# Three PSUM tiles in place of one: weighted values, second layer's narrow half and projection, with the pairs of banks in another order

## Chip, cores and metric

One Trainium2 chip (trn2), one core. The metric is the device time of one execution in microseconds, median of several executions.

In the profile PE is TensorE, which does the matmuls; DVE is VectorE, ACT ScalarE and POOL GpSimd. PEld stands for PE's weight loads. The matmuls write into PSUM, which is handled in banks. The granted clock is the share of TensorE's full clock that the trace shows as granted. A line such as `PE s L92 <- ACT o L536: 88.6, 62, 1.5` says that PE, about to write tile s at line 92 of the kernel, waited for ACT's operation on o at line 536: 88.6 us in total, 62 times, 1.5 us at most.

## What is computed

The reference works on x of shape 16 x 192 x 56 x 56 (float32). Cut to what matters here:

```python
# layer 0: shifted-window attention (7x7 windows, 6 heads of 32) and a two-layer perceptron
h   = roll(ln(x^T), (-3, -3));  win = windows(h)                   # 49 tokens each
q, k, v = split(win @ qkv_w + qkv_b)
out = softmax(q k^T * scale + bias + mask) v @ proj_w + proj_b
x1  = x + roll(unwindow(out), (3, 3))^T
x2  = x1 + (gelu(ln(x1^T) @ fc1_w + fc1_b) @ fc2_w + fc2_b)^T
# layer 1: depthwise 3x3 convolution, of which 4 taps are not masked; the taps depend on the image
t   = relu(bn(mean(x2, (2, 3)) @ w1.T));  wt = t @ w2.T + b2
out = depthwise_conv(x2, wt * MASK) + bias
```

The 192 channels are handled as 128 + 64. The "wide half" of a result is that of the 128 channels, the "narrow half" that of the 64. Each of the 64 steps handles one band of windows in two halves of the image, and four steps make an image.

## The kernel before

The kernel uses eight banks of PSUM as four pairs, each a tile of two banks, and the loop passes the pairs round under the names A, B_, C and D. All operations are issued in the order of the program. `mm` is the helper at line 92, so nearly all matmuls carry that line; tell them apart by their tiles (ph: first layer, pf: second layer, po: weighted values, pp: projection, pv: values of the next step, s: the shared tile).

```python
def banks(name, k):                       # one tile = one pair of banks
    return psum.tile([128, 2, 512], F32, tag=f"pair{k}", name=name)

def bank(k):
    return singles[0][:, k]
...
def attention_values(i, prts, k):
    po = banks(f"po_{i}", k)
    for wp in range(4):
        attention_weigh(po, bank(1), wp, prts[wp])      # a third of it into bank(1)
    return po[:, 0], po[:, 1], bank(1)

def project(i, o, k):
    pp = banks(f"pp_{i}", k)
    pp1 = bank(1)                                       # narrow half
    ...
def mlp_narrow(hid, pf1):  ...                          # second layer, narrow half
def taps(b, pooled):
    pt = bank(0)  ...                                   # taps of the convolution
```

The part of a step that the change touches (`mlp_out` is DVE's sum into x at L631, `conv_rest` the convolution's operations on DVE, `attention_rows` ACT's copies of the weighted values at L536):

```python
    pf = mlp_wide(i - 2, hid, B_, turn)
    mlp_out(i - 2, 0, pf[:, :, :T])
    ...
    singles[0] = banks(f"s_{i}", C)                     # the shared tile
    if has(i):
        o = attention_rows(i, attention_values(i, prts, D))
    mlp_narrow(hid, bank(0))
    for c in ys:
        conv_rest(*c)
    mlp_out(i - 2, 1, bank(0)[:, :T])
    if has(i):
        pp, pp1, p_narrow, p_rest, p_whole = project(i, o, A)
        p_narrow()
        p_rest()
    if has(i + 1):
        pvs, v_rest, v_whole = attention_v(i + 1, (B_, D))
        v_rest()
    if (i - 2) % STEPS == STEPS - 1:
        ...  taps(b, taps_pool(b))
    if has(i):
        p_whole()
        residual(i, pp, pp1)
    if has(i + 1):
        v_whole()
        attention_v_out(pvs)                            # copies that free the values' banks
    ...
    pairs = [C, A, B_, D]
```

## Time and profile before

| | before |
|---|---|
| median time | 3428.45 us (4 runs) |
| PE busy in the profiled run | 3183.9 us of 3430.2, 93% |
| PE idle | 246.3 us |
| of it: waits on the shared tile in the loop | 145.3 us |

The last row is the sum of 88.6 (on ACT o), 52.2 (on DVE's L631) and 4.5 us (on the taps' tt). PE busy and PE idle together are the span. The windows of two successive steps, from one narrow projection to the next (length, then busy time of PE, of its weight loads, of DVE, ACT and POOL, each with its number of instructions, then the granted clock, the share of DMA and its GB/s):

```profile
1705.35:1756.44 51.09, 48.76 (x415) 29.95 (x415) 34.30 (x60) 29.20 (x47) 11.46 (x10) 1.00 0.12 33
1756.44:1807.34 50.90, 48.76 (x414) 29.94 (x414) 25.85 (x54) 27.50 (x45) 11.70 (x11) 1.00 0.25 71
```

PE does the same 48.76 us of work in each step and idles for the rest.

### The profile page before, as it was taken

The page shows a single profiled execution, that of the slowest core. Times are in us where ns is not written, and L with a number is a line of the kernel's source. Part 1 is how long each engine was busy: PE and PEld are TensorE (multiplying, and loading weights), DVE is VectorE, ACT ScalarE, POOL GpSimd, SP SyncE. Part 2 cuts the span into 40 slices and gives each one's busy share as a digit, 9 for nine tenths or more (in the row PEclk, how much of TensorE's full clock was granted, in tenths as well). Part 3 has the DMA queues.
Part 4 walks back from the last instruction along what each step waited for, and adds up shares of the span by engine and source line. Part 5 has one row for each costly group of instructions (what it writes and reads, how often), then busy time and mean ns, then how long its engine had stood idle before and what let it go on. Part 6 is the DMA issues. An engine that isn't in the chain of part 4 may idle for free.

```text
span 3430.2 us, 64894 instructions
## 1 busy us (share of the span) xinstructions
PE 3183.9 (93%) x26642; PEld 1955.5 (57%) x26642; DVE 2078.5 (61%) x3893; ACT 1854.5 (54%) x2988; POOL 759.8 (22%) x656
## 2 busy tenths in 40 slices
PE   5799999999999999999999999999999999999996
PEld 3455555555555555555555555555555555555553
DVE  4354675665665665665665666665665656666564
ACT  3354564565565565565565565565565565555552
POOL 4211212212212212212212212212212222222220
PEclk7799999999999999999999999999999999999998
DMA  3101102111111102101111201102111110201001
GB/s 94 19 10 48 29 25 57 34 48 34 51 27 38 53 26 61 29 27 55 34 51 31 59 23 35 53 29 58 29 30 52 34 54 28 62 22 32 25 29 43
DMA packets 79124, 135.39 MB, mean 39 GB/s; under 512 B 21766, under 2 KB 61692, under 8 KB 76908
## 3 DMA queue, kind: packets, MB, share of 16 engines
q1 hardware_dynamic: 77266, 128.54, 13.3%
q8 instruction: 210, 3.44, 0.4%
q0 software_dynamic: 1056, 1.92, 0.3%
q10 hardware_dynamic: 506, 0.79, 0.1%
q14 instruction: 86, 0.70, 0.1%
HBM read 41.25 MB, written 38.54 MB: 23 GB/s over the span
## 4 chain that ended last, share of the span: by engine, by line
PE 84%; ACT 7%; DVE 4%; issue 1%; POOL 0%; DMA 0%; SPq 0%; DVEq 0%; POOLq 0%; ACTq 0%
PE ph L92 23%; PE pf L92 15%; PE s L92 10%; PE pv L92 7%; PE st L92 5%; PE pq L92 4%; PE pp L92 4%; PE sc L92 4%; PE pe L92 4%; PE pk L92 4%; PE pt L500 3%; ACT o L536 2%; ACT prt L506 2%; ACT L235 2%; DVE y L688 2%
## 5 line engine op out<-in xcount | busy, mean ns | idle before, releaser
L92 PE MATMUL ph<-yn,wf 128*128 128x392 f32 (+1 forms) x3072 | 802.3, 498 | 6.1 <-ACT vbd L443 3.3
L487 POOL TENSOR_TENSOR prob<-e,tot 113x588 f32<-113x588 f32 x256 | 297.8, 1174 | 1966.6 <-DVE tot L486 1966.6
L92 PEld LDWEIGHTS ph<-yn,wf 128*128 128x128 f32 (+1 forms) x3072 | 429.4, 189 | 350.6 <-issue 87.2
L443 ACT COPY vbd<-pv 49x192 f32<-49x192 f32 x512 | 135.4, 312 | 888.7 <-DVE vbd L441 888.5
L92 PE MATMUL pf<-hid,wf 128*128 128x392 f32 x1536 | 538.3, 494 | 3.5 <-ACT hid L588 2.0
L688 DVE SCALAR_TENSOR_TENSOR y<-x,wt,y 128x770 f32<-128x770 f32 x288 | 328.1, 1141 | 288.1 <-ACT y L673 281.4
L588 ACT ACTIVATE hid<-ph,f1b 128x784 f32<-128x784 f32 x384 | 336.8, 912 | 137.7 <-PE ph L92 137.7
L92 PEld LDWEIGHTS pf<-hid,wf 128*128 128x128 f32 x1536 | 281.5, 190 | 183.7 <-ACT hid L588 3.3
L92 PE MATMUL s<-hid,wf 128*64 128x392 f32 x1536 | 266.9, 496 | 88.6 <-ACT o L536 88.6
L92 PEld LDWEIGHTS pv<-wqkv,win 64*128 64x128 f32 (+1 forms) x2048 | 259.7, 190 | 39.6 <-ACT kbd L393 2.8
L471 DVE TENSOR_TENSOR e<-sc,bias_t 113x588 f32<-113x588 f32 x256 | 179.5, 761 | 168.0 <-PE sc L92 167.8
L92 PE MATMUL pv<-wqkv,win 64*128 64x192 f32 (+1 forms) x2048 | 274.0, 327 | 3.3 <-ACT kbd L393 2.5
L478 DVE TENSOR_TENSOR e<-e,top 113x588 f32<-113x588 f32 x256 | 266.5, 1041 | 8.9
L338 POOL TENSOR_TENSOR yn<-x,dv 128x784 f32<-128x784 f32 x64 | 132.0, 2063 | 565.4 <-DMA dv<-dev 537.8
L235 ACT ACT_TABLE_LOAD x192 | 246.3, 1283 | 3.4
L506 ACT COPY prt<-pt 128x678 f32<-128x678 f32 x256 | 179.1, 726 | 117.5 <-PE pt L500 116.0
L481 ACT ACTIVATE e<-e 113x588 f32<-113x588 f32 x256 | 176.8, 691 | 108.7 <-DVE e L478 108.7
L92 PEld LDWEIGHTS s<-hid,wf 128*64 128x64 f32 x1536 | 104.5, 137 | 216.2 <-issue 119.9
L441 DVE COPY vbd<-pv 49x192 f32<-49x192 f32 x512 | 159.1, 349 | 97.0 <-ACT vbd L443 83.0
L500 PEld LDWEIGHTS pt<-ident,prob 113*128 113x128 f32 x1536 | 167.3, 142 | 74.4 <-issue 45.3
L500 PE MATMUL pt<-ident,prob 113*128 113x113 f32 x1536 | 182.7, 262 | 10.3 <-ACT prt L506 8.5
L92 PE MATMUL po<-prt,vbd 128*64 128x49 f32 x4096 | 191.5, 225 | 0.2 <-ACT prt L506 0.2
(157 smaller groups left out, 4688.9 us busy)
## 6 DMA issues: line engine op xcount, KB each, us to landing
dv<-dev SPq DMA_DIRECT2D x1020, 49.0 KB
x<-in_x_dram SPq DMA_DIRECT2D x15, 1484.0 KB
out_dram<-y SPq DMA_DIRECT2D x48, 392.0 KB
out_dram<-y SPq DMA_DIRECT2D x48, 196.0 KB
x<-in_x_dram SPq DMA_DIRECT2D x16, 392.0 KB
x<-in_x_dram SPq DMA_DIRECT2D x15, 350.0 KB
out_dram<-y SPq DMA_DIRECT2D x16, 308.0 KB
out_dram<-y SPq DMA_DIRECT2D x16, 154.0 KB
```

The lines of the kernel that those rows point to most:

```text
L92: nc.tensor.matmul(dst, lhs, rhs, start=start, stop=stop, skip_group_check=True)
L235: nc.scalar.activation(junk, eps_t[0:1], func)
L441: nc.vector.tensor_copy(dst, f)
L443: nc.scalar.copy(dst, f)
L471: nc.vector.tensor_tensor(e, sc[:PW, :, : HEADS * N], rel, ALU.add)
L478: nc.vector.tensor_tensor(ehs[wp], ehs[wp], t.broadcast_to([PW, 2 * HEADS, N]), ALU.subtract)
L481: nc.scalar.activation(es[wp], es[wp], AF.Exp)
L487: nc.gpsimd.tensor_tensor(prob[wp][:PW, :, 0:N], ehs[wp], t.broadcast_to([PW, 2 * HEADS, N]), ALU.mult)
L500: nc.tensor.transpose(pt[:, a, g * PW : (g + 1) * PW], prob[wp][:PW, h : h + 2, :].rearrange("p h k -> p (h k)"), ident[:PW, :PW],)
L506: nc.scalar.copy(prt, pt[:, :, : 3 * PW])
L588: nc.scalar.activation(hid[:, f], phs[f][:, :, :T], AF.Gelu, bias=f1b[:, f : f + 1])
L688: nc.vector.scalar_tensor_tensor(dst, src, wt[:, kc, t : t + 1], dst, ALU.mult, ALU.add)
```

## The change

The intent is to take away the two waits of PE per step that come from one tile serving three purposes. The weighted values' third part (po1), the second layer's narrow half (pf1) and the narrow projection (pp1) each get a tile. So that there are pairs for them, the wide projection moves from A to B_, the next step's values from (B_, D) to (D, A), the taps behind the values, and the pairs go round in another order. The core of the diff:

```diff
-    def attention_values(i, prts, k):
-        po = banks(f"po_{i}", k)
+    def attention_values(i, prts, k, k1):
+        po, po1 = banks(f"po_{i}", k), banks(f"po1_{i}", k1)[:, 0]
...
-    def project(i, o, k):
-        pp = banks(f"pp_{i}", k)
-        pp1 = bank(1)
+    def project(i, o, k, k1):
+        pp, pp1 = banks(f"pp_{i}", k), banks(f"pp1_{i}", k1)[:, 0]
...
-    def mlp_narrow(hid, pf1):
+    def mlp_narrow(i, hid, k):
+        pf1 = banks(f"pf1_{i}", k)[:, 0]
...
-    def taps(b, pooled):
-        pt = bank(0)
+    def taps(b, pooled, k):
+        pt = banks(f"t_{b}", k)[:, 0]
...
-        singles[0] = banks(f"s_{i}", C)
         if has(i):
-            o = attention_rows(i, attention_values(i, prts, D))
-        mlp_narrow(hid, bank(0))
+            o = attention_rows(i, attention_values(i, prts, D, C))
+        pf1 = mlp_narrow(i - 2, hid, A)
...
-            pp, pp1, p_narrow, p_rest, p_whole = project(i, o, A)
+            pp, pp1, p_narrow, p_rest, p_whole = project(i, o, B_, C)
...
-            pvs, v_rest, v_whole = attention_v(i + 1, (B_, D))
+            pvs, v_rest, v_whole = attention_v(i + 1, (D, A))
             v_rest()
-        if (i - 2) % STEPS == STEPS - 1:
-            convs.append({"b": b, "n": 0, "wt": taps(b, taps_pool(b))})
         if has(i):
             p_whole()
             residual(i, pp, pp1)
         if has(i + 1):
             v_whole()
+        if (i - 2) % STEPS == STEPS - 1:
+            convs.append({"b": b, "n": 0, "wt": taps(b, taps_pool(b), C)})
+        if has(i + 1):
             attention_v_out(pvs)
...
-        pairs = [C, A, B_, D]
+        pairs = [C, B_, D, A]
```

(Cut: the two steps of the prologue, where the same tiles are separated in pair 3, and lines that only pass the new names on.)

More of the change, by code (lines that the diff above doesn't have):

```diff
@@ L523, in attention_weigh @@
                 )
-    def attention_values(i, prts, k):
-        po = banks(f"po_{i}", k)
+    def attention_values(i, prts, k, k1):
+        po, po1 = banks(f"po_{i}", k), banks(f"po1_{i}", k1)[:, 0]
         for wp in range(4):
-            attention_weigh(po, bank(1), wp, prts[wp])
-        return po[:, 0], po[:, 1], bank(1)
+            attention_weigh(po, po1, wp, prts[wp])
+        return po[:, 0], po[:, 1], po1
     def attention_rows(i, pos):
@@ L613, in mlp_narrow @@
                 )
+        return pf1
     def mlp_wide(i, hid, k, turn):
@@ L747, in tail_of @@
         if o is not None:
-            pp, pp1, narrow, rest, whole = project(i, o, kp)
+            pp, pp1, narrow, rest, whole = project(i, o, kp, 3)
             narrow()
@@ L949, in tile_swin_then_dynamic_conv @@
             f()
+        if i:
+            singles[0] = banks("singles", 3)
         for e in extra:
@@ L958, in tile_swin_then_dynamic_conv @@
         norm_squares(f"1_{i + 3}", i + 3, 0, nc.gpsimd)
-        o = attention_rows(i, attention_values(i, prts, 0))
+        o = attention_rows(i, attention_values(i, prts, 0, 3))
+        singles[0] = None
         tail_of(i, o, 1, (2, 0))
@@ L1036, in tile_swin_then_dynamic_conv @@
             norm_squares(f"1_{i + 3}", i + 3, 0, nc.gpsimd)
-        singles[0] = banks(f"s_{i}", C)
         if has(i):
-            o = attention_rows(i, attention_values(i, prts, D))
-        mlp_narrow(hid, bank(0))
+            o = attention_rows(i, attention_values(i, prts, D, C))
+        pf1 = mlp_narrow(i - 2, hid, A)
         for c in ys:
             conv_rest(*c)
-        mlp_out(i - 2, 1, bank(0)[:, :T])
+        mlp_out(i - 2, 1, pf1[:, :T])
         if has(i):
-            pp, pp1, p_narrow, p_rest, p_whole = project(i, o, A)
+            pp, pp1, p_narrow, p_rest, p_whole = project(i, o, B_, C)
             p_narrow()
@@ L1048, in tile_swin_then_dynamic_conv @@
         if has(i + 1):
-            pvs, v_rest, v_whole = attention_v(i + 1, (B_, D))
+            pvs, v_rest, v_whole = attention_v(i + 1, (D, A))
             v_rest()
-        if (i - 2) % STEPS == STEPS - 1:
-            b = (i - 2) // STEPS
-            convs.append({"b": b, "n": 0, "wt": taps(b, taps_pool(b))})
         if has(i):
@@ L1058, in tile_swin_then_dynamic_conv @@
             v_whole()
+        if (i - 2) % STEPS == STEPS - 1:
+            b = (i - 2) // STEPS
+            convs.append({"b": b, "n": 0, "wt": taps(b, taps_pool(b), C)})
+        if has(i + 1):
             attention_v_out(pvs)
```

## The prediction

> **What bounds the kernel now.** I read the page first, then the list of waits of TensorE, then PE's timeline in a few steps of the loop, then DVE's beside it. The page:
>
> ```profile
> span 3430.2 us, 64894 instructions
> PE 3183.9 (93%) x26642; PEld 1955.5 (57%) x26642; DVE 2078.5 (61%) x3893; ACT 1854.5 (54%) x2988; POOL 759.8 (22%) x656
> ...
> PE   5799999999999999999999999999999999999996
> ```
>
> PE is busy for 93% of the span, the next engine for 61%, and PE's row is at 9 in nearly all slices. So PE bounds, and only the 3430.2 - 3183.9 = 246.3 us in which it stands idle can be won: the change takes away no matmul and adds none. Who makes PE wait is in the waits of PE:
>
> ```profile
> PE s L92 <- ACT o L536: 88.6, 62, 1.5
> PE s L92 <- DVE x L631: 52.2, 62, 1.2
> PE singles L143 <- DMA cols_rows<-in_L_conv_qkv_b_dram: 10.0, 1, 10.0
> ...
> PE s L92 <- DVE tt L651: 4.5, 15, 0.3
> ```
>
> (columns: total us, times, longest). Two waits come once in each of the 62 loop steps that have an attention, 1.43 us and 0.84 us on average: 140.8 us of the 246. The rest of the list is single waits of the prologue and the end. Both waits are on the tile s: one PSUM tile of two banks that holds the last third of the weighted values (bank 1), the narrow half of the second layer (bank 0) and the narrow half of the projection (bank 1 again). PE's timeline of one step (start us, duration us, group, idle before and releaser):
>
> ```profile
> 1749.66 0.29 PE L92 MATMUL s<-prt,vbd 128*64 128x49 f32 x4
> 1751.43 4.17 PE L92 MATMUL s<-hid,wf 128*64 128x392 f32 x24 [1.48 <-ACT o L536]
> 1756.44 0.88 PE L92 MATMUL s<-o,wp 128*64 128x392 f32 x4 [0.84 <-DVE x L631]
> 1757.25 0.93 PE L92 MATMUL pp<-o,wp 64*128 64x392 f32 x4
> 1758.01 1.47 PE L92 MATMUL pv<-wqkv,win 64*128 64x192 f32 x16
> 1759.41 0.93 PE L92 MATMUL s<-o,wp 128*128 128x392 f32 x2
> 1760.17 1.48 PE L92 MATMUL pp<-o,wp 128*128 128x392 f32 x4
> 1761.48 2.76 PE L92 MATMUL pv<-wqkv,win 128*128 128x192 f32 x16
> ```
>
> The 24 matmuls of the second layer read only hid, ready long ago, and write bank 0. They wait until ACT has copied the weighted values out of bank 1. Then the projection, which needs only o (ACT was done with it 4 us earlier), waits until DVE has read bank 0. Neither wait is of data: both come from the tile being one. A step is about 51 us, and the windows of four successive steps show PE idle for 2.1 to 2.6 us in each, so there is nearly nothing else to win in the loop. The granted clock there is 1.00.
>
> **What the Trainium skill says.** "Perfetto Trace Analysis", section Optimization Strategy, says that a gap which repeats on the engine that should be saturated can mean too few buffers for the next tile; the trace agrees, 62 times each. The same page, section Matmuls, says that independent groups of matmuls should go round different PSUM banks, so that the evacuation of one overlaps the next: here the banks differ, and yet the trace shows the wait, so what counts is the tile that the program tracks. "PSUM — Partial Sum Buffer", section PSUM bank collisions raise a hardware error, asks for order by bank and quadrant, not for order between two banks; so the separated tiles need no wait in its place. "SBUF — State Buffer", section Who interferes with whom, says that a VectorE copy in a two-port mode and a GpSimd operation block each other wholly. The trace agrees: the row copy of the convolution, L697, takes 0.19 us, but 1.72 to 1.84 us when it meets POOL's yn.
>
> **The change, part by part.**
>
> (1) *The second layer's narrow half goes into the step's pair A*, last read by ACT's copy prt of the fourth window pair, which the weighted values need anyway. The wait on ACT o vanishes: 62 x 1.43 = 88.6 us. ACT's copies (1.2 us) then lie beside these 24 matmuls (4.17 us) and are done before the projection.
>
> (2) *The projection goes into B and C.* B was last read by DVE at L631 for the wide half (from 1745.88, 1.03 us: long past), C by ACT o. The wait on DVE vanishes: 62 x 0.84 = 52.2 us. Where groups follow without a wait, the next starts 0.07 to 0.17 us before the end of the one before (pp at 1757.25, s ended at 1757.32). Two such overlaps per step are won back: about 0.2 us x 62 = 12 us. That makes 153 us in all.
>
> (3) *The values of the next step go into D and A.* Their second half is the first thing that must now wait for DVE's L631 on A. PE reaches it the length of the projection's first parts and of half the values later: 0.81 + 0.76 + 0.70 = 2.3 us after the end of the second layer's half. In a step whose convolution has no row copy, DVE is free by then, and L631 takes 0.62 us: no wait. In the steps with a row copy that meets POOL, DVE is late:
>
> ```profile
> 1752.34 1.74 DVE L697 COPY y<-cols 64x56 f32<-64x56 f32 x1
> 1754.12 1.72 DVE L688 SCALAR_TENSOR_TENSOR y<-x,wt,y 128x770 f32<-128x770 f32 x1
> 1755.76 0.61 DVE L631 SCALAR_TENSOR_TENSOR x<-s,cols,x 128x392 f32<-128x392 f32 x1
> ```
>
> L631 ends at 1756.4. PE would be there at 1749.8 (weighted values out) + 4.0 + 2.3 = 1756.1, so it waits some 0.35 us. I counted 11 slow L697 in the loop: 4 us given back.
>
> (4) *The taps of the convolution move behind the values.* This comes in every fourth step, 15 times in the loop (the 16th is in the end). The matmuls themselves are as many. Before, they held the projection up by 0.94 us (1810.31 to 1811.25 in such a step), now they hold up the next step's first ph, which takes the same pair C: much the same. But in DVE's order they now stand before the copies that free the values' banks:
>
> ```profile
> 1810.99 0.21 DVE L651 TENSOR_TENSOR tt<-s,bn 128x48 f32<-128x48 f32 x1 [1.95 <-PE s L92]
> ...
> 1812.74 0.74 DVE L570 SCALAR_TENSOR_TENSOR x<-s,cols,x 128x371 f32<-128x371 f32 x2
> 1813.54 1.41 DVE L574 SCALAR_TENSOR_TENSOR x<-pp,cols,x 128x371 f32<-128x371 f32 x4
> 1814.86 0.60 DVE L441 COPY vbd<-pv 49x192 f32<-49x192 f32 x2
> ```
>
> From tt to the end of the taps is 1.75 us (1810.99 to 1812.74). The copies of the first half then take 2.45 us until ACT's part is done (1814.86 to 1817.31). Set the start of the taps' tt to 0: the pair D is free at 1.75 + 2.45 = 4.2. The first ph starts at about 0.25, and the third, which takes D, 2.64 later (8 matmuls of 0.33), at 2.9. PE waits 1.3 us. The late copies also push ACT's squares and first gelus back, for which the fifth and sixth ph wait a little, 0.3 us. 15 x 1.6 = 24 us given back.
>
> (5) *The new order of the pairs* keeps the roles of the next step: first the pair that the projection's narrow part leaves, then its wide part's, then the values'. The first is free after two DVE operations of 0.75 us in sum, while PE still has 1.3 + 2.6 us of other work. In a usual step the third ph finds its pair free 1.2 us early, before as after. Nothing is won or lost. The two prologue steps separate two tiles in the same pair; nothing.
>
> Sum: 153 - 24 - 4 = 125 us. 3428.9 - 125 = **3303 us**, 3.7% faster (a ratio of 1.038).
>
> **The rivals.** *DVE takes over*: every wait on L631 is only moved from the projection to the second half of the values, and the gain is part (1) and little of (2). For it: in the chain of waits some steps already run over ACT y, DVE y and L631, not over the second layer. Against it: DVE is 61% busy, L631 came at once after the matmuls in 51 of 64 cases (DVE waits 191.9 us there for PE), and PE has 2.3 us of other work first. If it held in the steps with a row copy, 29 x 1 us more would be lost: about 3330 us. *The taps cost nothing or much more*: if the copies keep up, 24 us less is lost and the time is 3280; if the delay runs on through the gelus and the next softmax, 3 us per such step or more, 3325. *Another wait takes the place of the ones removed*, since a step is 2.5 us shorter for all: the DMA of dv to POOL's yn and the next ph is the longest line beside PE. In the trace yn ends at 1860.1 and ph wants it at 1867, so 7 us of room shrinks to 4.5. Were all of the gain eaten, we would be at 3429; I see no sign of it. *The clock is throttled* by a PE that never stops: it is granted 1.00 at 95% already, so I don't expect it.
>
> **Range and chances.** If only the idle of the list is won and not the overlaps, 3316; with no loss at the taps, 3280; with DVE late in the steps with row copies, 3330. So 3280 to 3330 holds it 8 times in 10. Over 2% faster needs 67 us, half of the sum, and part (1) alone has 89: 0.96. Within 2%: 0.035. Slower needs a chain through a new buffer that I don't see: 0.005.
>
> **What would show each step right or wrong.** Right: PE's waits have no line for ACT o and none for L631 before the projection; the second layer's 24 matmuls start as the weighted values end; PE's busy time stays near 3184 and its idle falls to about 120; usual steps take about 48.6 us. Step (3): 11 or so waits of the values on L631, 0.3 us each. Step (4): some 15 waits of ph on ACT or DVE vbd, 1.3 us each, and taps steps 1.6 us longer than the matmuls added. Wrong: waits on L631 before the values in most steps; ph waiting for vbd, yn or the residual in every step; a clock under 1.00 in the loop.

## The result and the profile after

The changed kernel took 3291.36 us (median of 4 runs, 3289.66 to 3292.23), against 3428.45 us before. All outputs are right. Ratios here are the mean time of one kernel's runs over that of the other's runs of the same rounds, so they are not quite the ratio of the medians. This one is 0.9597, with a 95% interval of 0.958 to 0.9614.

The page of the changed kernel:

```profile
span 3290.4 us, 64877 instructions
PE 3164.4 (96%) x26642; PEld 1950.0 (59%) x26642; DVE 2053.2 (62%) x3893; ACT 1856.1 (56%) x2988; POOL 751.3 (23%) x656
```

The matmuls are as many as before (26642). The span fell by 139.8 us. PE's idle fell from 246.3 to 126.0 us, which is 120.3 of it. The other 19.5 us are of PE's busy time, without one matmul less: groups that follow without a wait overlap at their ends (by 0.17 us at each of the two places in the timeline below), and the groups behind a wait had taken 0.04 to 0.05 us longer.

The waits of PE in the changed kernel (total us, times, longest; lines have moved by one, so L632 is the L631 of before):

```profile
PE ph L92 <- ACT vbd L443: 18.8, 16, 3.3
...
PE ph L92 <- DVE tt L652: 5.9, 15, 0.4
PE pv L92 <- DVE x L632: 4.7, 12, 0.5
```

The waits on ACT o and on L631 before the projection are gone from the loop. Three small ones are new in the loop: ph for the copies of the values (one of the 16, 3.3 us long, is in the prologue and was there before), ph for the taps, and the values for L632. The prediction names all three, the second only as "much the same" as the hold-up that it replaces. PE's timeline of a usual step answers to the one that the prediction shows of before:

```profile
1677.45 3.08 PE L92 MATMUL po<-prt,vbd 128*64 128x49 f32 x96
1680.36 4.13 PE L92 MATMUL pf<-hid,wf 128*64 128x392 f32 x24
1684.32 1.69 PE L92 MATMUL pp<-o,wp 128*64 128x392 f32 x8
1685.85 1.47 PE L92 MATMUL pv<-wqkv,win 64*128 64x192 f32 x16
1687.24 2.24 PE L92 MATMUL pp<-o,wp 128*128 128x392 f32 x6
1689.32 2.76 PE L92 MATMUL pv<-wqkv,win 128*128 128x192 f32 x16
```

No line carries an idle in brackets, and each group starts a little before the end of the one above it. The windows of two steps and of a whole image of four steps:

```profile
1544.00:1740.42 196.42, 194.66 (x1664) 120.08 (x1662) 126.39 (x240) 115.21 (x186) 45.47 (x37) 1.00 0.15 42
1594.81:1643.75 48.94, 48.60 (x415) 29.93 (x415) 34.30 (x60) 29.23 (x47) 11.67 (x9) 1.00 0.11 34
1643.75:1692.09 48.34, 48.34 (x415) 29.97 (x415) 32.15 (x60) 29.25 (x47) 11.61 (x9) 1.00 0.18 44
```

A usual step takes 48.34 us, all of it busy, where it took 51.09. In the step of 48.94 us the values waited for L632. Four steps took 205.05 us before (the four pieces of the windows, 51.99 + 51.07 + 51.09 + 50.90) and take 196.42 us now.

What holds PE up in the step with taps shows in DVE's timeline and then in PE's:

```profile
1544.41 0.21 DVE L652 TENSOR_TENSOR tt<-t,bn 128x48 f32<-128x48 f32 x1 [1.09 <-PE t L92]
...
1546.08 0.17 DVE L667 TENSOR_TENSOR wt<-wt,b2t 128x8 f32<-128x8 f32 x1
1546.17 0.61 DVE L441 COPY vbd<-pv 49x192 f32<-49x192 f32 x2
```

```profile
1543.84 0.54 PE L92 MATMUL t<-w1t,pooled 128*128 128x48 f32 x4
1544.77 2.87 PE L92 MATMUL ph<-yn,wf 128*128 128x392 f32 x8 [0.39 <-DVE tt L652]
1548.67 5.90 PE L92 MATMUL ph<-yn,wf 128*128 128x392 f32 x28 [1.03 <-ACT vbd L443]
```

The copies start only at 1546.17, behind the taps' five operations, and the third ph (the ninth matmul) waits 1.03 us for them.

### The profile page after: what moved, and what is told of

It is laid out like the page before. It is cut to its first block, busy times and chain, and to the rows that moved or that the text cites. A ratio compares the mean times of both kernels' runs of the same rounds, so it can differ in the third digit from the quotient of the medians.

```text
span 3290.4 us, 64877 instructions
## 1 busy us (share of the span) xinstructions
PE 3164.4 (96%) x26642; PEld 1950.0 (59%) x26642; DVE 2053.2 (62%) x3893; ACT 1856.1 (56%) x2988; POOL 751.3 (23%) x656
## 4 chain that ended last, share of the span: by engine, by line
PE 88%; DVE 4%; ACT 2%; issue 2%; POOL 0%; DMA 0%; SPq 0%; POOLq 0%; ACTq 0%; DVEq 0%
PE ph L92 23%; PE pf L92 21%; PE pv L92 7%; PE pp L92 7%; PE st L92 5%; PE po L92 5%; PE pq L92 4%; PE pt L500 4%; PE sc L92 4%; PE pe L92 4%; PE pk L92 4%; DVE y L689 1%; DVE y L698 1%; DVE vbd L441 1%; ACT L235 1%
## 5 line engine op out<-in xcount | busy, mean ns | idle before, releaser
L92 PE MATMUL pf<-hid,wf 128*128 128x392 f32 (+1 forms) x3072 | 802.9, 494 | 3.5 <-ACT hid L587 2.0
L92 PEld LDWEIGHTS pf<-hid,wf 128*128 128x128 f32 (+1 forms) x3072 | 386.4, 164 | 303.6 <-issue 119.9
L689 DVE SCALAR_TENSOR_TENSOR y<-x,wt,y 128x770 f32<-128x770 f32 x288 | 320.3, 1114 | 282.1 <-ACT y L674 275.3
L92 PE MATMUL pp<-o,wp 128*128 128x392 f32 (+2 forms) x896 | 251.5, 514 | 2.7 <-ACT o L536 2.7
L632 DVE SCALAR_TENSOR_TENSOR x<-pf,cols,x 128x784 f32<-128x784 f32 (+1 forms) x128 | 105.8, 827 | 233.1 <-PE pf L92 218.9
L235 ACT ACT_TABLE_LOAD x192 | 246.3, 1283 | 3.4
L92 PE MATMUL po<-prt,vbd 128*64 128x49 f32 x6144 | 198.2, 224 | 0.0
L92 PEld LDWEIGHTS po<-prt,vbd 128*64 128x64 f32 x6144 | 190.2, 139 | 9.4 <-ACT prt L506 0.6
```

Source lines behind the costliest of these rows:

```text
L92: nc.tensor.matmul(dst, lhs, rhs, start=start, stop=stop, skip_group_check=True)
L235: nc.scalar.activation(junk, eps_t[0:1], func)
L689: nc.vector.scalar_tensor_tensor(dst, src, wt[:, kc, t : t + 1], dst, ALU.mult, ALU.add)
```

## The experiments

They ran in three sessions, on one chip each, and in each the kernel before ran beside them; its medians there were 3429.5 to 3430.1 us. The change itself had run beside a kernel before of 3428.45 us, so 1 to 2 us between it and another row say nothing. The theory is the prediction's: PE bounds, both waits come from the shared tile and not from data, and small losses are given back. The rivals are that DVE's chain takes over, that the losses have other causes, and that the order of the pairs is free.

| run | median us | ratio to before (95% interval) |
|---|---|---|
| the change | 3291.36 | 0.9597 (0.958 to 0.9614) |
| part (1) alone | 3366.08 | 0.9819 (0.98 to 0.9839) |
| part (1) alone, convolution behind L631 | 3343.45 | 0.9751 (0.9735 to 0.9767) |
| part (2) alone | 3362.4 | 0.9802 (0.9785 to 0.9818) |
| change, taps at their old place | 3269.67 | 0.9533 (0.9518 to 0.9547) |
| change, taps' DVE work split | 3268.54 | 0.9527 (0.9513 to 0.9541) |
| change, taps beside the projection | 3259.4 | 0.9502 (0.9488 to 0.9516) |
| change, row copy on ACT | 3285.61 | 0.9581 (0.9567 to 0.9595) |
| change, taps beside, row copy on ACT | 3252.96 | 0.9485 (0.9471 to 0.9499) |
| change, values' pair first | 3422.26 | 0.998 (0.9963 to 0.9997) |
| the same, taps beside the projection | 3366.89 | 0.9819 (0.9805 to 0.9834) |

### Part (1) alone

The second layer's narrow half leaves the tile of the weighted values; the narrow projection shares its new tile.

```diff
+        singles[0] = banks(f"n_{i}", B_)
         mlp_narrow(hid, bank(0))
...
-            pvs, v_rest, v_whole = attention_v(i + 1, (B_, D))
+            pvs, v_rest, v_whole = attention_v(i + 1, (D, C))
...
-        pairs = [C, A, B_, D]
+        pairs = [B_, A, D, C]
```

> The kernel before with part (1) alone: the second layer's narrow half leaves the tile of the weighted values and goes to the pair of its wide half; the narrow projection shares its tile, so the wait on DVE's L631 stays. Theory (both waits come from shared tiles, and DVE stays just behind PE): the wait of the second layer on ACT o is gone in all 62 steps, worth 1.55 us in about 51 of them and nothing where a slow row copy (11 in the trace) makes DVE late, since the projection then waits for DVE until the old moment: 3428.5 - 79 = about 3349 us. Rival (DVE's chain of the convolution is the bound behind the wait): PE stands at L631 as long as it stood at ACT o, and the time stays above 3400 us.

Measured: 3366.08 us, 17 us more than expected, and not the rival's 3400 either. The wait on ACT o is gone from the list of PE's waits, which shows that it came from the shared tile. But the wait on L631 grew from 52.2 to 84.0 us:

```profile
PE n L92 <- DVE x L631: 84.0, 64, 2.8
```

In 40 of the 62 steps it is 0.83 or 0.90 us, in 22 it is 1.25 us and more. One of the 22, on DVE and on POOL:

```profile
1721.40 0.19 DVE L697 COPY y<-cols 64x56 f32<-64x56 f32 x1
1721.62 2.50 DVE L688 SCALAR_TENSOR_TENSOR y<-x,wt,y 128x770 f32<-128x770 f32 x1
1724.05 0.61 DVE L631 SCALAR_TENSOR_TENSOR x<-n,cols,x 128x392 f32<-128x392 f32 x1
```

```profile
1721.45 1.86 POOL L338 TENSOR_TENSOR yn<-x,dv 128x784 f32<-128x784 f32 x1 [8.41 <-DMA dv<-dev]
```

Here the row copy L697 is fast, and it is the convolution's last tap L688 that takes 2.50 us in place of 1.02. POOL's yn had begun 0.17 us earlier and ended at 1723.31; 0.81 us of the tap are left after that, somewhat less than its usual length. The expectation had counted only slow row copies, 11 of them (the trace of the kernel before has 10). The Trainium skill, "SBUF — State Buffer", section Who interferes with whom, says that a VectorE instruction with two SBUF inputs contends with a GpSimd instruction that reads SBUF; L688 reads x and y from SBUF, so this is that case, and the trace agrees.

The long waits cost more than their length. After eight of them, of 1.98 to 2.75 us, the granted clock was 0.50 for 3.41 us, as in this window that begins 0.5 us behind such a wait:

```profile
464.59:468.00 3.41, 3.41 (x18) 2.22 (x16) 0.00 (x0) 0.00 (x0) 2.05 (x2) 0.50 0.32 104
```

The work from the projection to the next ph took 9.15 to 9.29 us in these eight steps, in place of 7.65: 13 us in all.

### Part (1) alone, with the convolution behind L631

```diff
-        for c in ys:
-            conv_rest(*c)
         mlp_out(i - 2, 1, bank(0)[:, :T])
+        for c in ys:
+            conv_rest(*c)
```

> The kernel with part (1) alone, which came out at 3366 us in place of 3349, now with DVE's L631 ahead of the convolution's three operations in place of behind them. In the run of part (1) alone the wait on L631 was 0.8 to 0.9 us in 40 steps and 1.25 to 2.75 us in 22, where an operation of the convolution had met POOL's yn. Theory (DVE's lateness by POOL ate the rest of the gain): no wait on L631 over 1 us, 0.9 us in all 62 steps: 62 x 1.55 = 96 us less than the kernel before, 3332 us. Rival (the convolution behind L631 delays the residual and the copies of the values, and ph waits in place of it): 3345 us or more, with waits of ph on vbd or x.

Measured: 3343.45 us, 23 us less than part (1) alone but 11 us over the theory's figure and just under the rival's.

```profile
PE n L92 <- DVE x L631: 58.1, 64, 1.3
```

The long waits are gone and with them the falls of the clock in the loop; 59 of the 62 waits are 0.83 or 0.90 us. So DVE's lateness did eat two thirds of what was missing (23 of 34 us). Of the last 11 us, the rival explains most. The list of PE hides it, as ph waits on vbd there only 3 times (3.8 us, 3.3 of it in the prologue), but the list of its weight loads shows it:

```profile
PEld ph L92 <- ACT hid L588: 21.9, 54, 0.5
PEld ph L92 <- ACT vbd L443: 12.7, 25, 0.9
```

Neither line is in the list of part (1) alone. In 26 of 61 steps the 36 ph take 8.28 to 8.96 us and not 8.26: 8 us in sum, in gaps too short to be listed as waits. So the late convolution does delay the copies of the values and the gelus, and gives this much back.

### Part (2) alone

```diff
         if has(i):
+            singles[0] = banks(f"p_{i}", B_)
             pp, pp1, p_narrow, p_rest, p_whole = project(i, o, A)
...
-            pvs, v_rest, v_whole = attention_v(i + 1, (B_, D))
+            pvs, v_rest, v_whole = attention_v(i + 1, (D, C))
...
-        pairs = [C, A, B_, D]
+        pairs = [B_, A, D, C]
```

> The kernel before with part (2) alone: the narrow projection gets its own pair, the second layer's narrow half stays in the tile of the weighted values and waits for ACT o. Theory: the 62 waits on L631 before the projection go, 1.05 us each with the overlap of the matmuls, and no new wait of the values on L631, as they come 2.3 us later: 3428.5 - 65 = about 3363 us, 1.4 us of wait on ACT o left per step. Rival (the wait is only moved to the values): 3410 to 3429 us.

Measured: 3362.4 us, as the theory said. The first line of PE's waits is the other part's, untouched:

```profile
PE s L92 <- ACT o L536: 88.5, 62, 1.5
```

No wait of pv on L631 is in the list, so the rival, a wait moved to the values, falls. The two parts alone save 1.8% and 2.0%; the change with the taps at their old place saves 4.7%, more than the sum. In part (1) alone the projection still stood behind a late DVE in 22 steps. Together with part (2) it doesn't wait for L631 at all, and the 2.3 us until the values cover most of that lateness. The sums agree: with the lateness taken away, as in the run above, part (1) saves 86 us; part (2) saves 68, together 154, and the change with the taps at their old place 160.

### The taps at their old place

In the changed kernel, before the projection's last matmuls, in the second bank of pp1's tile (diffs of the taps are shortened here and below, with some conditions in words):

```diff
+        if (i - 2) % STEPS == STEPS - 1:
+            convs.append({..., "wt": taps(b, taps_pool(b), C, pp1_tile(i))})
         if has(i):
             p_whole()
...
-        if (i - 2) % STEPS == STEPS - 1:
-            convs.append({..., "wt": taps(b, taps_pool(b), C)})
```

> The changed kernel, with part (4) undone: taps in the second bank of the narrow projection's tile and before its last matmuls, as in the kernel before. Theory: 15 waits of ph for vbd (1 us) and for tt (0.4 us) vanish and 15 waits of the projection on tt (0.3 us) come back; a step with taps costs 0.9 us more than a usual one in place of 2.46: 3291.4 - 23 = about 3268 us. Rival (the wait for vbd has another cause, such as ACT or the shorter step): the 16 waits stay and the time stays at 3288 to 3292.

Measured: 3269.67 us, 22 us less than the change. The waits of ph for vbd and tt in the loop are gone but for one of 0.2 us, and the old one is back:

```profile
PE pp L92 <- DVE tt L659: 4.5, 15, 0.3
```

### The taps' DVE work split

```diff
-            convs.append({..., "wt": taps(b, taps_pool(b), C)})
+            pt = banks(f"t_{b}", C)[:, 0]
+            taps_mm(b, taps_pool(b), pt)
+            tt = taps_read(b, pt)           # the one read of PSUM
         if has(i + 1):
             attention_v_out(pvs)
+        if tt is not None:                  # the other four operations
+            convs.append({..., "wt": taps_rest(b, tt)})
```

> The changed kernel, with only DVE's order changed: the one read of the taps' PSUM stays where it is, the other four operations of the taps go behind the copies of the values. Theory: the wait of the third ph on vbd (1.03 us idle) goes, the wait of the first ph on tt (0.39 us) stays: some 15 x 1.4 = 21 us less, 3270 us. Rival (it is the place of the matmuls or the pair C and not the four operations): 3291 us.

Measured: 3268.54 us. Nothing on PE was moved, and the wait on vbd went while the one on tt stayed, so the loss of part (4) is the four operations ahead of the copies on DVE:

```profile
PE ph L92 <- DVE tt L652: 5.9, 15, 0.4
```

### The taps beside the projection

```diff
+        if last step of the image:
+            pooled = taps_pool(b)                       # sums ready while DVE is idle
+            pt = second bank of pp1's tile
         if has(i):
             p_whole()
+        if pooled is not None:
+            taps_mm(b, pooled, pt)
         if has(i):
             residual(i, pp, pp1)
+        if pooled is not None:
+            tt = taps_read(b, pt)
         ...                                             # v_whole, attention_v_out
+        if pooled is not None:
+            convs.append({..., "wt": taps_rest(b, tt)})
```

> The changed kernel with the taps' matmuls right after the projection's, in the second bank of its narrow tile, sums made ready beforehand; DVE reads them after the residual and does the rest after the copies of the values. Theory: no wait of PE left at the taps, only 0.4 us of matmuls: 15 x 2.05 = 31 us less than the changed kernel, 3261 us. Rival (the residual now waits for the taps' matmuls, 0.4 us later, and the copies with it, so that the third ph waits): 3270 us or more.

Measured: 3259.4 us, 32 us less than the change. PE's timeline at the taps:

```profile
1526.32 2.24 PE L92 MATMUL pp<-o,wp 128*128 128x392 f32 x6
1528.39 0.54 PE L92 MATMUL pp<-w1t,pooled 128*128 128x48 f32 x4
1528.77 2.83 PE L92 MATMUL pv<-wqkv,win 128*128 128x192 f32 x16
1531.44 8.26 PE L92 MATMUL ph<-yn,wf 128*128 128x392 f32 x36
```

The taps cost their 0.4 us and no wait. The rival (a later residual holds up the third ph) falls.

### The row copy on ACT

```diff
-            nc.vector.tensor_copy(
+            nc.scalar.copy(
                 y[p, LAST - 3 * PR, :], cbk[p].broadcast_to([p.stop - p.start, IMG])
```

> The changed kernel with the convolution's row copy L698 on ACT in place of DVE, so that it cannot meet POOL[...]. Theory: the 12 waits of the values on L632 (4.7 us idle in all, some 7 with the lost overlap of the matmuls) go: 3285 us. Rival (the waits on L632 come from elsewhere, or ACT's copy and two semaphores make DVE late in all 29 such steps): 3291 us or more.

Measured: 3285.61 us, about 6 us less than the change. The intervals of the two ratios overlap, so the time alone doesn't settle it; but the waits of the values on DVE's sum into x are gone from the list, and the next run shows the same 6 us within one session. So the row copy that meets POOL is the cause of part (3)'s loss.

### Both mends together

> Both mends together, the taps beside the projection and the row copy on ACT. If they add up: 3291.4 - 31 - 6 = about 3254 us, PE without a wait of the loop's own longer than 0.1 us. If they do not, 3261 us as with the taps alone.

Measured: 3252.96 us (3252.32 to 3255.24), against 3259.4 us (3256.0 to 3261.56) with the taps alone in the same session. The mends add up. In a window of 200 us of the loop PE is busy all the time:

```profile
1600.00:1800.00 200.00, 200.00 (x1683) 123.84 (x1682) 135.19 (x248) 120.94 (x197) 48.19 (x40) 1.00 0.15 41
```

This is faster than both kernels. In this stretch no wait is left to win.

### The values' pair first in the order

```diff
-        pairs = [C, B_, D, A]
+        pairs = [D, B_, C, A]
```

> The changed kernel with another order of the pairs for the next step: the values' first pair D comes first, the projection's narrow pair third. Theory: the first ph then waits in every step for the copies of the values, 1.45 us in a usual step and some 2.3 us more than now in a step with taps: 47 x 1.45 + 15 x 2.3 = 103 us more, about 3394 us, most of the gain of the change lost. Rival (the order is free, as DVE and ACT catch up): 3291 us.

Measured: 3422.26 us; nearly the whole gain is gone, so the order is not free. But it is 28 us more than expected. The waits of ph on the copies are 46 of 1.31 us and 15 of 4.33 or 4.34 us, about as expected. What follows a long one was not (windows, then PE's timeline of another such step):

```profile
1602.30:1606.62 4.32, 0.00 (x0) 0.03 (x1) 3.46 (x11) 1.06 (x4) 0.00 (x0) 0.89 0.01 2
1606.62:1609.00 2.38, 2.38 (x4) 1.42 (x5) 1.75 (x5) 1.58 (x5) 0.00 (x0) 0.50 0.00 0
1609.00:1612.00 3.00, 3.00 (x6) 1.40 (x6) 1.77 (x10) 0.75 (x2) 0.00 (x0) 0.50 0.00 0
1612.00:1615.00 3.00, 3.00 (x13) 1.58 (x13) 0.00 (x0) 0.36 (x1) 0.00 (x0) 0.92 0.00 0
```

```profile
1813.76 10.03 PE L92 MATMUL ph<-yn,wf 128*128 128x392 f32 x36 [4.34 <-DVE vbd L441]
```

The granted clock falls to 0.50 within the gap of 4.3 us and stays there for 5.8 us of work in this case; it falls at each of the 15 long gaps, in 13 of them for 3.41 us. The 36 ph take 10.03 us in those 13 (11.23 in the step of the windows, 10.66 in one), and 8.34 us after a gap of 1.31 us. Over the 15 that is 27 us. The accounts agree: against the change PE's idle is 101 us more in the profiled run, as expected (103), and its busy time 29 us more.

### The same order, with the taps beside the projection

> The wrong order of the pairs together with the taps beside the projection. The wrong order came out at 3422 us in place of 3394; behind the 15 waits of 4.34 us at the taps the granted clock was 0.5 for some us and 36 ph took 10.0 us in place of 8.3. Theory (the long gap costs once more by the clock): with the taps moved no gap is over 1.5 us, the clock stays at 1.00 in the loop, and a step costs 1.5 us more than with the right order: 3259.4 + 62 x 1.5 = 3352 us. Rival (the clock falls or ph is slow for another reason, such as the late gelus): 3375 us or more, with ph at 10 us in some steps.

Measured: 3366.89 us, 15 us over the theory's figure.

```profile
PE ph L92 <- DVE vbd L441: 90.6, 61, 2.0
```

The 15 waits at the taps are 2.0 us and not the assumed 1.5, as the taps' matmuls and read now stand ahead of the residual; that is 7 us of the 15. Behind 12 of them the 36 ph take 8.34 us at a clock of 1.00. But behind three the clock fell once more, against the theory, and ph took 10 us, the rival's mark:

```profile
572.48 10.03 PE L92 MATMUL ph<-yn,wf 128*128 128x392 f32 x36 [2.02 <-DVE vbd L441]
```

```profile
569.00:572.51 3.51, 1.49 (x10) 1.23 (x9) 2.78 (x11) 1.06 (x4) 0.00 (x0) 1.00 0.00 0
572.51:575.92 3.41, 3.41 (x6) 1.81 (x7) 2.70 (x8) 2.33 (x6) 0.00 (x0) 0.50 0.00 0
```

(Over the whole loop the clock's mean still prints as 1.00.) That is 5 us more; the last 3 are not settled. Shorter gaps took away 12 of the 15 falls, so the gap is their cause, but a gap of 2 us isn't safe. When a fall comes can be read from the clock's record in the traces: all its changes lie on a grid of 3.41 us. In the loops of all runs the clock fell 26 times (8 in part (1) alone, 15 and 3 in the two runs of this order), each time after a stretch of that grid in which PE stood idle for 1.98 us or more, and it never fell after one with 1.96 us or less. A gap of 2.02 us falls wholly into one stretch only sometimes, here 3 times of 15.

## Why the prediction was right

**What bounds the kernel** held, with two slips. PE's idle is most of what was won, and the clock in the loop stayed at 1.00. But the prediction said that only the 246.3 us of idle can be won and, as a sign of being right, that PE's busy time stays near 3184 us; it fell to 3164.4, and its own 12 us for the overlap could come from nowhere else. Its idle of about 120 us (measured: 126.0) doesn't follow from its own sum either, which gives 246.3 - 140.8 + 28 = 133.5.

**Part (1) and part (2)** held. Both waits vanished, and each vanished alone when its tile was separated. They were expected to give 140.8 us of idle. The accounts agree: the idle on the shared tile was 145.3 us with the taps' 4.5, the new waits in the loop are 26.1 us (15.5 on vbd, 5.9 on tt, 4.7 on L632), so the idle should fall by 119.2 us, and it fell by 120.3.

**The overlap of the groups** is the term that was mis-sized: 0.2 us per step or 12 us in the sum, while PE's busy time in a usual step fell by 0.42 us (48.76 to 48.34), which is 26 us in 62 steps; 19.5 us are left of it, since each new wait costs its overlap again. A usual step takes 48.34 us where the prediction said about 48.6. This is most of the difference between 3303 and 3291.

**Part (3)** held: 12 waits of about 0.4 us where 11 of 0.35 us were foreseen (the trace of before has 10 slow row copies and not 11, that of the change 12), and 6 us came back when the row copy left DVE. Its reason was incomplete: the convolution's taps collide with POOL as well, which the 2.3 us of other work on PE hide in the change and part (1) alone does not.

**Part (4)** held: 15 waits of 1.03 us on the copies (1.3 foreseen), and of 0.39 us on tt in place of the old 0.30; a loss of 22 us by the run with the taps at their old place, 24 predicted. The late gelus are there too: PE's weight loads wait for ACT hid in ph 30 times, which they did not before, and hold the ph up by 0.16 us in the step with taps that was looked at (0.3 foreseen). The run with the split work confirms the mechanism, the taps' operations ahead of the copies.

**Part (5)** held: the order that keeps the roles costs nothing (with both mends PE waits nowhere in a stretch of 200 us), and the one tried that does not costs 131 us, 27 of them by the clock.

**The rivals.** DVE doesn't take over in the change, but it does eat a part of the gain where only part (1) is done. No wait takes the place of those removed except the three that were counted and the short one of the weight loads. One rival was not tested: each separated tile also lies in another pair of banks, and no run changed the tile and kept the pair.

## What to carry to other kernels

Where the engine that bounds waits once per step for a reader of a bank that it isn't going to touch, look at which tile the wait is tied to: giving each purpose its own tile took away the wait without touching the work. Then ask of every reuse what the bounding engine meets first, and keep operations that nobody waits for behind the copies that free its next buffer. An idle of that engine that comes back in every step costs its own length and the overlap of the groups around it; one of 2 us or more could cost the clock afterwards too. And look at such falls one by one: a mean over the loop hides them.

## What the Trainium skill lacked or had wrong

- No page that I read tells of a wait between two different banks of one tile. "PSUM — Partial Sum Buffer", section PSUM bank collisions raise a hardware error, asks for order by bank and quadrant only; yet with both banks in one tile PE waited 62 times for 1.43 us and 62 times for 0.84 us, and separate tiles removed both. That these waits are the program's and not the hardware's is argued, from the tiles alone: each new tile is also in another pair of banks.
- "Perfetto Trace Analysis", section Matmuls, advises to rotate through different banks; it lacks what the tile does to this. Here different banks of one tile did not overlap; with separate tiles, in other pairs of banks, the same matmuls took 4.0% less time.
- "TensorE: Matmul & The Clock Gate", section HAM oscillation, asks for no idle of PE over about 3.4 us. That is too wide here: gaps of 4.34 us brought the granted clock to 0.50 each time, but so did gaps of 1.98 to 2.75 us in 11 cases; in the loops gaps of up to 1.97 us never did, and some longer ones didn't either. It gives the price of a gap for a kernel of matmuls alone; in this mixed one it was 1.5 to 2.9 us on top of the gap.
- "SBUF — State Buffer", section Who interferes with whom, is right on both forms seen here: a row copy of 0.19 us took 1.72 to 1.89 us when it was slow (before and after the change), and an instruction of 1.02 us with two inputs in SBUF took 2.50 us beside POOL's yn.
